# A two-layer row-and-column scan on one core: passes of one layer and eight batches, packed row steps, borders moved under the neighbouring scans

## Chip, cores and metric

The kernel runs on one core of one Trainium2 chip. The metric is the time of one execution on the device, in microseconds (us).

## What is computed

The input is 32 batches of 48 channels x 64 rows x 128 columns, float32. Each of two layers normalizes its input in 16 groups of three channels (over the group's channels, rows and columns of one batch), runs four scans over the result and adds what comes out to its input. A scan step adds a 5-tap convolution of the line before to the next line; all 48 channels mix. Down and up go along the rows with the same weights (the convolution runs along the 128 columns), right and left along the columns (the convolution runs along the 64 rows).

```
def step(w, b):
    def f(carry, inp):
        nxt = inp + _conv1d(carry, w, b)      # 48 x 48 x 5 taps, padding 2, and a bias
        return (nxt, nxt)
    return f
...
_, d_rest = jax.lax.scan(step(down_w, down_b), d0, xs[1:])        # 63 steps over rows
...
_, u_rest = jax.lax.scan(step(down_w, down_b), u0, seq)           # 63 steps back
...
_, r_rest = jax.lax.scan(step(right_w, right_b), r0, ws[1:])      # 127 steps over columns
...
_, l_rest = jax.lax.scan(step(left_w, left_b), l0, R[Ww - 2::-1]) # 127 steps back
...
x = x + _L0_conv_ref(_gn(x), ...)
x = x + _L1_conv_ref(_gn(x), ...)
```

## The kernel before

Partitions 0 to 47 hold the channels of even positions and 64 to 111 those of odd ones (`SIDES`, P = 112), so that a product of 112 x 112 weights handles two positions of a convolution at once. A chain is four batches (`G`); there are eight chains in two lanes, and `run_lane` is written as a generator, of which the loop at the end (L260 to L262) takes a step of one lane and then of the other. Each lane does its chain's first layer, the border to the second layer, the second layer and the border to the next chain, four chains one after the other.

A step (`step`, L169) is three TensorE products over the same moving line, shifted by none, one back and one ahead (L174, L175, L178), into one accumulator, and one VectorE addition of accumulator, bias and input line (L181). In down and up a line is 64 positions x 4 batches = 256 values a partition, in right and left 32 x 4 = 128. A float32 product is two passes, each with its own weight load, so every product appears as two instructions. In up, ScalarE also copies each new line to its place in the column layout (`place`, L189).

At a border (the end of `run_lane`) each of the four batches of a lane is handled in turn: GpSimd adds the scan's result to the input tile (`add_scan`, L107), SP stores it to `mid` or `out` (L104), and `stats` computes the next layer's statistics of it on VectorE (L120 to L146, with two small products L124 and L131 and a square root L136), after which `normalize` writes the map, one half on ScalarE (L153) and one on GpSimd (L160). After the second layer the tile is first loaded with a new batch (L99). Two input tiles a lane (`NX`) are loaded 25 steps ahead of the end of left (`early`). All input and output DMAs stand in SP's queue and move 512-byte runs.

The order of each engine's instructions is fixed when the program is built, from the dependences; an engine takes its queue in that order and waits where something is not ready.

Of the kernel before, what the change touches and what calls it, by code (L numbers as in the profile page):

```python
# [21 lines left out]
F32 = mybir.dt.float32  # L23
# [9 lines left out]
G = 4  # L33
LANES = 2
NX = 2
DOWN, RIGHT, LEFT = range(3)
SIDES = (slice(0, C), slice(ODD, ODD + C))
# [3 lines left out]
def kernel(  # L41
# [10 lines left out]
    HP, WP = H // 2, W // 2  # L52
    NCHAINS = B // G
    SEG = 512
    NSEG = HP * W // SEG

    cpool = ctx.enter_context(tc.tile_pool(name="cpool", bufs=1))
    carry_pool = ctx.enter_context(tc.tile_pool(name="carry", bufs=2))
    stat_pool = ctx.enter_context(tc.tile_pool(name="stat", bufs=2))
    dram = ctx.enter_context(tc.tile_pool(name="dram", bufs=1, space=bass.MemoryType.DRAM))  # L60
    ps_scan = ctx.enter_context(
        tc.tile_pool(name="ps_scan", bufs=3, space=bass.MemoryType.PSUM)
# [5 lines left out]
    w_sb = cpool.tile([P, 2, 3, 3, P], F32, tag="w_sb", name="w_sb")  # L68
    b_sb = cpool.tile([P, 2, 3], F32, tag="b_sb", name="b_sb")
    mask_sb = cpool.tile([P, P], F32, tag="mask_sb", name="mask_sb")  # L70
    xts = [
        [cpool.tile([P, HP, W], F32, tag=f"x{i}_{k}", name=f"x{i}_{k}") for k in range(NX)]
        for i in range(LANES)
    ]
    maps = [
        cpool.tile([P, WP, 2, HP, G], F32, tag=f"map{i}", name=f"map{i}")
        for i in range(LANES)
    ]
    lasts = [
        cpool.tile([P, WP, G], F32, tag=f"last{i}", name=f"last{i}") for i in range(LANES)  # L80
    ]
    mid = dram.tile([B, C, H, W], F32, tag="mid", name="mid")


    for i, t in enumerate(maps + [xt for lane in xts for xt in lane]):
        eng = nc.vector if i % 2 else nc.gpsimd
        eng.memset(t[32:64], 0.0)
    nc.scalar.dma_start(mask_sb, mask)
    nc.scalar.dma_start(b_sb, bias)
    nc.scalar.dma_start(w_sb, w)  # L90

    def rows(ap: bass.AP, b: int, side: int) -> bass.AP:
        return ap[b].rearrange("c (q r) w -> r c q w", r=2)[side]

    def load_x(lane: int, src: bass.AP, b: int) -> bass.AP:

        xt = xts[lane][b % G % NX]
        for side in range(2):
            nc.sync.dma_start(xt[SIDES[side]], rows(src, b, side))  # L99
        return xt  # L100

    def store_x(dst: bass.AP, b: int, xt: bass.AP):
        for side in range(2):
            nc.sync.dma_start(rows(dst, b, side), xt[SIDES[side]])  # L104

# [5 lines left out]
    def stats(xt: bass.AP, key: str):  # L111


        def small(n, name):
            return stat_pool.tile([P, n], F32, tag=name, name=f"{name}_{key}")
# [200 lines left out]
```

## Time and profile before

| | |
|---|---|
| median of the runs | 7141.41 us (3 runs, 7123.3 to 7152.01) |
| the profiled execution | 7140.95 us |
| its span, first to last instruction | 7139.2 us |
| mean granted TensorE clock | 0.88 |
| TensorE matmul busy | 5473.6 us (77%) |
| VectorE, ScalarE, GpSimd busy | 3006.9, 1402.4, 1279.8 us |
| moved by DMA | 258.09 MB, 497403 packets |

Busy time is that of instructions in flight; the engines overlap, so the shares don't add up to the span. PE is TensorE's matmuls, PEld its weight loads, DVE VectorE, ACT ScalarE, POOL GpSimd, SP the queue that issues most DMAs. PEclk is the clock that was granted to TensorE, as a share of 2.4 GHz. In a timeline a row's bracket tells how long the engine had been idle and whose end released it.

### The profile page before, as it was taken

How to read it: one execution, taken by the hardware profiler on the slowest of the kernel's cores; microseconds unless marked ns; L12 is line 12 of the kernel's file. 1: busy time of each engine (PE TensorE's matmuls, PEld its weight loads, DVE VectorE, ACT ScalarE, POOL GpSimd, SP SyncE). 2: the span in 40 equal slices, each digit the busy share in tenths (PEclk: the TensorE clock that was granted, in tenths of full speed). 3: DMA queues.
4: the chain of work that ended last, by engine and by line, in shares of the span. 5: the costliest groups of instructions: out<-in, count | busy, mean ns of one | idle time of the engine just before them, and what ended most of it. 6: DMA issues, size and time to landing. Idle time of an engine off the chain costs nothing. (4 is left out here: it accounts for less than half of the span.)

```text
span 7139.2 us, 85243 instructions
## 1 busy us (share of the span) xinstructions
PE 5473.6 (77%) x36736; PEld 4951.8 (69%) x36736; DVE 3006.9 (42%) x7235; ACT 1402.4 (20%) x2241; POOL 1279.8 (18%) x199
## 2 busy tenths in 40 slices
PE   3999549993399945999339994599923999459992
PEld 2889538993289943899328994489922899448992
DVE  5345523452334553345223455334522345533451
ACT  3230213201323021320122302132012230213200
POOL 5000440004400044000440004300043000530004
PEclk9999769996699976999669997799966999779996
DMA  9000350006800035000590003500058000340006
GB/s 111 1 1 1 51 91 1 1 1 88 124 1 1 1 54 88 1 1 1 89 124 1 1 1 57 85 1 1 1 89 123 1 1 1 62 80 1 1 1 106
DMA packets 497403, 258.09 MB, mean 36 GB/s; under 512 B 5392, under 2 KB 496912, under 8 KB 497024
## 3 DMA queue, kind: packets, MB, share of 16 engines
q1 hardware_dynamic: 496640, 251.68, 24.4%
q8 instruction: 287, 4.70, 0.3%
q10 hardware_dynamic: 384, 0.96, 0.1%
q14 instruction: 92, 0.75, 0.0%
HBM read 151.95 MB, written 100.66 MB: 35 GB/s over the span
## 5 line engine op out<-in xcount | busy, mean ns | idle before, releaser
L107 POOL TENSOR_TENSOR x<-x,map 112x4096 f32<-112x4096 f32 x64 | 693.6, 10850 | 5310.1 <-issue 2639.2
L124 PE MATMUL ps_stat_x<-mv_x,mask_sb 112*112 112x1 f32 x64 | 16.5, 327 | 713.9 <-DVE mv_x L122 707.9
L124 PEld LDWEIGHTS ps_stat_x<-mv_x,mask_sb 112*112 112x112 f32 x64 | 15.0, 288 | 717.4 <-DVE mv_x L122 710.4
L124 PE MATMUL ps_stat_m<-mv_m,mask_sb 112*112 112x1 f32 x64 | 16.5, 327 | 479.9 <-DVE mv_m L122 454.6
L136 ACT ACTIVATE std_m<-var_m 112x1 f32<-112x1 f32 x32 | 6.5, 203 | 1841.6 <-DVE var_m L133 1841.5
L120 DVE BATCH_NORM_STATS2 st_x<-x 112x6 f32<-112x512 f32 x256 | 155.6, 679 | 499.6 <-DMA x<-in_x 499.3
L124 PEld LDWEIGHTS ps_stat_m<-mv_m,mask_sb 112*112 112x112 f32 x64 | 15.0, 287 | 483.6 <-DVE mv_m L122 456.8
L160 POOL TENSOR_SCALAR map<-x,scale_x,offset_x 48x2048 f32<-48x2048 f32 x64 | 284.4, 4443 | 333.6 <-DVE offset_x L146 327.7
L136 ACT ACTIVATE std_x<-var_x 112x1 f32<-112x1 f32 x32 | 6.5, 203 | 1596.3 <-DVE var_x L133 1596.2
L160 POOL TENSOR_SCALAR map<-x,scale_m,offset_m 48x2048 f32<-48x2048 f32 x64 | 281.0, 4390 | 193.0 <-DVE offset_m L146 169.1
L120 DVE BATCH_NORM_STATS2 st_m<-x 112x6 f32<-112x512 f32 x256 | 160.5, 679 | 348.3 <-POOL x L107 348.3
L153 ACT ACTIVATE map<-x,offset_x,scale_x 48x2048 f32<-48x2048 f32 x64 | 282.8, 4419 | 43.8 <-DVE offset_x L146 40.3
L153 ACT ACTIVATE map<-x,offset_m,scale_m 48x2048 f32<-48x2048 f32 x64 | 280.5, 4383 | 50.5 <-DVE offset_m L146 33.1
L189 ACT COPY map<-last 48x256 f32<-48x256 f32 x32 | 12.9, 403 | 1251.8 <-DVE last L181 1251.5
L131 PE MATMUL ps_stat_m<-sq_m,mask_sb 112*112 112x1 f32 x64 | 16.6, 329 | 153.1 <-DVE sq_m L130 153.1
L131 PEld LDWEIGHTS ps_stat_m<-sq_m,mask_sb 112*112 112x112 f32 x64 | 14.3, 285 | 157.1 <-DVE sq_m L130 157.1
L130 DVE SCALAR_TENSOR_TENSOR sq_m<-dev_m,mv_m 112x1 f32<-112x1 f32 x32 | 78.1, 2439 | 0.7
L181 DVE SCALAR_TENSOR_TENSOR map<-ps_1L0r,b_sb,map 112x128 f32<-112x128 f32 x127 | 44.6, 351 | 44.6 <-PE ps_1L0r L178 44.6
L181 DVE SCALAR_TENSOR_TENSOR map<-ps_7L0r,b_sb,map 112x128 f32<-112x128 f32 x127 | 44.6, 351 | 44.5 <-PE ps_7L0r L178 44.5
L181 DVE SCALAR_TENSOR_TENSOR map<-ps_5L0r,b_sb,map 112x128 f32<-112x128 f32 x127 | 44.6, 351 | 44.5 <-PE ps_5L0r L178 44.5
L181 DVE SCALAR_TENSOR_TENSOR map<-ps_3L0r,b_sb,map 112x128 f32<-112x128 f32 x127 | 44.6, 351 | 44.3 <-PE ps_3L0r L178 44.3
L181 DVE SCALAR_TENSOR_TENSOR map<-ps_3L1r,b_sb,map 112x128 f32<-112x128 f32 x127 | 44.6, 351 | 44.2 <-PE ps_3L1r L178 44.2
(617 smaller groups left out, 17240.0 us busy)
## 6 DMA issues: line engine op xcount, KB each, us to landing
x<-in_x SPq DMA_DIRECT2D x128, 768.0 KB, 16.2
mid<-x SPq DMA_DIRECT2D x64, 768.0 KB, 12.0
x<-mid SPq DMA_DIRECT2D x64, 768.0 KB, 16.1
out<-x SPq DMA_DIRECT2D x64, 768.0 KB, 12.6
w_sb<-in_w ACTq DMA_DIRECT2D x1, 882.0 KB, 12.3
mask_sb<-in_mask ACTq DMA_DIRECT2D x1, 49.0 KB, 1.9
b_sb<-in_b ACTq DMA_DIRECT2D x1, 2.6 KB, 5.4
```

Of the source, the lines that this page charges most:

```text
L107: nc.gpsimd.tensor_tensor(xt, xt, maps[lane][:, :, :, :, j].rearrange("c p r q -> c q (p r)"), ALU.add)
L120: nc.vector.bn_stats(st[:, s, :], flat[:, bass.ts(s, SEG)])
L124: nc.tensor.matmul(ps[:, 0:1], mask_sb, mv[:, 0:1], start=True, stop=True)
L130: nc.vector.scalar_tensor_tensor(sq, dev, dev, mv[:, 1:2], ALU.mult, ALU.add)
L131: nc.tensor.matmul(ps[:, 1:2], mask_sb, sq, start=True, stop=True)
L136: nc.scalar.activation(std, var, AF.Sqrt)
L153: nc.scalar.activation(maps[lane][SIDES[0], :, hs, :, j], view[hsl, :, 0, :], AF.Identity, bias=offset[hsl], scale=scale[hsl],)
L160: nc.gpsimd.tensor_scalar(maps[lane][SIDES[1], :, hs, :, j], view[hsl, :, 1, :], scale[hsl], offset[hsl], ALU.mult, ALU.add,)
L181: nc.vector.scalar_tensor_tensor(dst, ps, b_sb[:, layer, way : way + 1], inp, ALU.add, ALU.add)
L189: nc.scalar.copy(maps[lane][SIDES[hs], :, ws, q, :], carry[SIDES[ws]])
```

## The change

The work is cut differently. A pass is one layer of eight batches (`GB`), and there are eight passes: four of the first layer, then four of the second. There is one chain at a time.

- Down and up: eight neighbouring positions of a line x 48 channels are packed into 384 = 3 x 128 partitions (`PIECES`, `NG`), so a line is three groups of 128 values. A step (`row_step`) is nine 128 x 128 products in the order of `PRODUCTS` (input group, output group, shift) into three accumulators, with one VectorE addition for each group behind its last product. Results are written in place.
- Right and left: as before, but the two interleaved chains are the two halves of the eight batches (`col_step`).
- Rows and columns share one region (`arena`): the rows begin at its start, the columns 20 rows later (`SHIFT`). In up, each eight finished rows are moved to the column layout by 20 DMAs (`hand_over`); ScalarE's copies are gone.
- `prepare` brings eight batches of x to DRAM in the order that the rows want (load, statistics, GpSimd reordering, store, in 16 pieces); it runs for the first eight batches ahead of everything and for the others while a pass of the first layer is in right. `fetch` loads rows by ten DMAs and normalizes them in place by 24 ScalarE activations.
- The rows 0 to 19 of the next pass are loaded during left (three `fetch`). The residual of a pass (`drain`, 16 pieces) and the other six `fetch` are written among the down steps of the next pass. In the first layer a piece of the residual adds on GpSimd, stores to `mid` and computes statistics; in the second it adds and stores to `out`.
- Weights of the row steps are placed by 62 DMAs a layer, on ScalarE's queue at the start and on SP's during right of the fourth pass.

The new functions, cut to their core, and the driving loop (`collect` is one statistics instruction for each batch; `scaling` is the work of `stats` for eight batches at once, with four small products; the functions `load_x`, `store_x`, `add_scan`, `stats`, `normalize`, `step`, `place`, `scan` and `run_lane` go):

```
-G = 4
-LANES = 2
-NX = 2
+GB = 8
+HB = GB // 2
+E8 = 8
+FULL = 128
+NG = E8 * C // FULL
+SHIFT = 20
+CH = 2
+RB = 8
+LOADS = tuple(slice(a, b) for a, b in ((0, 4), (4, 12), (12, 20))) + tuple(
+    slice(a, min(a + 8, 64)) for a in range(20, 64, 8)
+)
+EARLY = 3
+PRODUCTS = (
+    (0, 0, 0),
+    (0, 1, 0),
+    (1, 0, 0),
+    (1, 1, 0),
+    (2, 0, -1),
+    (2, 1, 0),
+    (1, 2, 0),
+    (0, 2, 1),
+    (2, 2, 0),
+)
...
+    arena = const([FULL, SHIFT * ROW + HP * PAIR], "arena")
+    rows = arena[:, 0 : H * ROW].rearrange("p (h o n) -> p h o n", h=H, o=NG)
+    cols = arena[0:P, SHIFT * ROW :].rearrange(
+        "p (q e k b) -> p q e k b", q=HP, e=E8, k=NK
+    )
...
+    def prepare(g: int):
...
+        for j in range(NCH):
+            nat, perm = nats[j % 2], perms[j % 2]
...
+                nc.sync.dma_start(
+                    nat[SIDES[s]],
+                    x[g * GB : (g + 1) * GB, :, h : h + CH].rearrange(
...
+            collect(st, j, nat, f"x{g}_{j}")
...
+            for r in range(CH):
+                nc.gpsimd.tensor_copy(perm5[:, r], nat[:, r])
...
+                nc.sync.dma_start(
+                    stages[0][g][h : h + CH].rearrange("h c n -> c h n"), perm[SIDES[s]]
+                )
+            yield
+        return scaling(st, f"x{g}")
+
+    def fetch(layer: int, g: int, j: int, scale, offset):
+
+        hs = LOADS[j]
+        src = stages[layer][g][hs].rearrange("h c (e n) -> e c h n", e=E8)
+        for e, c0, c1, o, p0 in PIECES:
+            nc.sync.dma_start(rows[p0 : p0 + c1 - c0, hs, o], src[e][c0:c1])
+        view = rows[:, hs].rearrange("p h o (k b) -> p o b h k", b=GB)
+        for o in range(NG):
+            for b in range(GB):
+                nc.scalar.activation(
...
+    def hand_over(j: int):
+
+        qs = slice(RB // 2 * j, RB // 2 * (j + 1))
+        for r in range(2):
+            src = rows[:, RB * j : RB * (j + 1)].rearrange("p (q r) o n -> r o p q n", r=2)
+            dst = cols[SIDES[r], qs].rearrange("p q e k b -> e p q (k b)")
+            for e, c0, c1, o, p0 in PIECES:
+                nc.sync.dma_start(dst[e][c0:c1], src[r, o][p0 : p0 + c1 - c0])
+
+    def residual(layer: int, g: int, q: int, i: int, st):
...
+        for r in range(2):
+            nc.sync.dma_start(nat[SIDES[r]], src[r, :, q : q + CH])
+        res = cols[:, q : q + CH].rearrange("p q e k b -> p q (e k b)")
+        if layer == 0:
+            nc.gpsimd.tensor_tensor(res, res, nat, ALU.add)
...
+                nc.sync.dma_start(dst[r, :, q : q + CH], res[SIDES[r]])
+            collect(
...
+        else:
+            for t in range(CH):
+                nc.gpsimd.tensor_tensor(
+                    perm[:, t].rearrange("p (b k e) -> p b k e", b=GB, k=NK),
...
+    def row_step(layer: int, key: str, prev, inp, dst):
...
+        for n, (i, o, s) in enumerate(PRODUCTS):
+            seen[o] += 1
+            a, b = max(0, -s) * GB, N - max(0, s) * GB
+            nc.tensor.matmul(
+                ps[o][:, a:b],
+                wd[:, n],
+                prev[:, i, a + s * GB : b + s * GB],
...
+            if seen[o] == left[o]:
+                nc.vector.scalar_tensor_tensor(
+                    dst[:, o], ps[o], bd[:, layer, o : o + 1], inp[:, o], ALU.add, ALU.add
+                )
...
+    def drain(n: int):
...
+        first = (H - SHIFT) * ROW // (CH * PAIR) + 1
+        order = list(range(first)) + list(range(NCH - 1, first - 1, -1))
+        loads = list(range(EARLY, len(LOADS))) if n + 1 < len(passes) else []
+        for i, j in enumerate(order):
+            residual(layer, g, CH * j, i, st)
+            free = SHIFT + (i + 1) * CH * PAIR // ROW
+            while loads and (i >= first or LOADS[loads[0]].stop <= free):
+                fetch(*passes[n + 1], loads.pop(0), *coeffs[passes[n + 1]])
+            yield
+        if layer == 0:
+            coeffs[1, g] = scaling(st, f"m{g}")
...
+    load_row_weights(0, nc.scalar)
+    load_col_weights(0, nc.scalar)
+    for _ in drive(prepare(0), (0, 0)):
+        pass
+    for j in range(len(LOADS)):
+        fetch(0, 0, j, *coeffs[0, 0])
+
+    for n, (layer, g) in enumerate(passes):
...
+        for stage, i in scans(n):
+            if stage in ("down", "up") and left_over:
+                t = i if stage == "down" else 2 * H - 2 - i
+                due = t % 2 == 0 if t <= 18 else t % 6 == 0
+                if due and next(left_over, "end") == "end":
+                    left_over = None
+            if stage == "right":
+                if ahead and i % 7 == 0 and next(ahead, "end") == "end":
+                    ahead = None
+                if i == 1 and nxt and nxt[0] != layer:
+                    load_row_weights(nxt[0], nc.sync)
+            if stage == "left" and nxt and i % 32 == 31 and i < 96:
+                fetch(*nxt, 2 - i // 32, *coeffs[nxt])
+        if nxt and nxt[0] != layer:
+            load_col_weights(nxt[0], nc.sync)
+    for _ in drain(len(passes) - 1):
+        pass
```

## Rows read from the trace of the kernel before

**Rows 1.** The page's 40 slices, in tenths: granted clock, DMA engines.
```profile
PEclk9999769996699976999669997799966999779996
DMA  9000350006800035000590003500058000340006
```

**Rows 2.** Table of stretches: head, rows, columns, border, border, tail; column names first.
```profile
core 0: us, PE busy (x) PEld busy (x) DVE busy (x) ACT busy (x) POOL busy (x), PEclk, DMA share, GB/s
0.00:135.60 135.60, 20.95 (x59) 14.09 (x59) 91.16 (x151) 67.12 (x25) 85.60 (x23) 1.00 1.23 128
135.60:459.20 323.60, 322.94 (x1487) 265.18 (x1488) 119.25 (x247) 105.97 (x255) 4.12 (x1) 1.00 0.08 9
459.20:800.20 341.00, 340.61 (x3049) 340.19 (x3047) 178.35 (x508) 0.99 (x3) 0.04 (x1) 1.00 0.00 1
800.20:1001.50 201.30, 23.83 (x66) 15.76 (x65) 89.09 (x150) 67.77 (x24) 152.71 (x23) 0.51 0.61 97
...
1663.30:1917.10 253.80, 20.93 (x59) 14.12 (x59) 60.92 (x149) 69.21 (x24) 154.24 (x24) 0.51 0.95 141
7008.20:7139.20 131.00, 0.00 (x1) 0.00 (x0) 0.35 (x1) 0.00 (x0) 86.59 (x8) 0.52 0.87 144
```

**Rows 3.** Timeline of a step in right: start us, us, engine, line, operation.
```profile
600.23 0.38 PE L178 MATMUL ps_1L0r<-map,w_sb 112*112 112x124 f32 x2
...
600.44 0.38 PE L174 MATMUL ps_0L0r<-map,w_sb 112*112 112x128 f32 x2
...
600.65 0.35 DVE L181 SCALAR_TENSOR_TENSOR map<-ps_1L0r,b_sb,map 112x128 f32<-112x128 f32 x1 [0.35 <-PE ps_1L0r L178]
600.66 0.38 PE L175 MATMUL ps_0L0r<-map,w_sb 112*112 112x124 f32 x2
...
601.05 0.27 PEld L174 LDWEIGHTS ps_1L0r<-map,w_sb 112*112 112x112 f32 x2
```

**Rows 4.** The page's groups (busy us, mean ns), and one of down.
```profile
L107 POOL TENSOR_TENSOR x<-x,map 112x4096 f32<-112x4096 f32 x64 | 693.6, 10850 | 5310.1 <-issue 2639.2
L160 POOL TENSOR_SCALAR map<-x,scale_x,offset_x 48x2048 f32<-48x2048 f32 x64 | 284.4, 4443 | 333.6 <-DVE offset_x L146 327.7
L189 ACT COPY map<-last 48x256 f32<-48x256 f32 x32 | 12.9, 403 | 1251.8 <-DVE last L181 1251.5
L181 DVE SCALAR_TENSOR_TENSOR map<-ps_1L0r,b_sb,map 112x128 f32<-112x128 f32 x127 | 44.6, 351 | 44.6 <-PE ps_1L0r L178 44.6
...
L181 DVE SCALAR_TENSOR_TENSOR map<-ps_1L0d,b_sb,map 112x256 f32<-112x256 f32 x46 | 22.3, 484 | 36.7 <-PE ps_1L0d L178 36.7
```

**Rows 5.** Timeline at a border's end: lane 0 scans again, lane 1 is not ready.
```profile
976.21 10.89 POOL L107 TENSOR_TENSOR x<-x,map 112x4096 f32<-112x4096 f32 x1
...
979.62 0.48 DVE L181 SCALAR_TENSOR_TENSOR map<-ps_0L1d,b_sb,map 112x256 f32<-112x256 f32 x1 [2.97 <-PE ps_0L1d L178]
...
987.14 4.84 DVE L120 BATCH_NORM_STATS2 st_m<-x 112x6 f32<-112x512 f32 x8 [7.04 <-POOL x L107]
991.90 0.47 DVE L181 SCALAR_TENSOR_TENSOR map<-ps_0L1d,b_sb,map 112x256 f32<-112x256 f32 x1
...
992.42 1.19 PE L174 MATMUL ps_0L1d<-map,w_sb 112*112 112x256 f32 x2 [9.39 <-DVE map L181]
```

**Rows 6.** Timeline at the start of that border: GpSimd's additions, VectorE's small operations.
```profile
800.15 43.27 POOL L107 TENSOR_TENSOR x<-x,map 112x4096 f32<-112x4096 f32 x4 [660.43 <-issue]
...
822.73 0.63 DVE L120 BATCH_NORM_STATS2 st_m<-x 112x6 f32<-112x512 f32 x1
...
824.11 8.53 DVE L128 TENSOR_TENSOR dev_m<-mv_m,mean_m 112x1 f32<-112x1 f32 x1
```

**Rows 7.** The page's DMA queues (packets, MB, share), and the timeline of one issue.
```profile
q1 hardware_dynamic: 496640, 251.68, 24.4%
q8 instruction: 287, 4.70, 0.3%
...
1.16 0.45 ACTq L89 DMA_DIRECT2D b_sb<-in_b  x1
```

**Rows 8.** Table of stretches, columns as in rows 2: lane 0 alone, then both lanes.
```profile
996.60:1001.40 4.80, 4.07 (x8) 2.14 (x8) 0.69 (x3) 4.45 (x2) 4.38 (x1) 0.50 0.86 171
...
1004.80:1011.00 6.20, 5.19 (x23) 3.62 (x23) 2.27 (x5) 0.59 (x1) 0.85 (x1) 0.99 1.14 163
```

More of the change, by code (lines that the diff above doesn't have):

```diff
@@ L177, in step @@
         )
         nc.tensor.matmul(
-            ps[:, 0 : n - 1], wt[:, 2], prev[:, 1:n], start=False, stop=True
+            ps[:, 0 : HP - 1], wt[:, 2], prev[:, 1:HP], start=False, stop=True
         )
         nc.vector.scalar_tensor_tensor(
-            dst, ps, b_sb[:, layer, way : way + 1], inp, ALU.add, ALU.add
+            dst, ps, bc[:, layer, way : way + 1], dst, ALU.add, ALU.add
         )
-    def place(lane: int, h: int, carry: bass.AP):
-        q, hs = divmod(h, 2)
-        for ws in range(2):
-            nc.scalar.copy(maps[lane][SIDES[hs], :, ws, q, :], carry[SIDES[ws]])
@@ L191, in scan @@
-    def scan(lane: int, layer: int, key: str, early):
-        m, last = maps[lane], lasts[lane]
-        def row(h):
-            return m[:, :, h % 2, h // 2, :]
-        def col(v):
-            return m[:, v // 2, v % 2, :, :]
-        for h in range(1, H):
-            dst = row(h) if h < H - 1 else last
-            step(lane, layer, DOWN, f"{key}d{h}", row(h - 1), row(h), dst)
-            yield
-        place(lane, H - 1, last)
-        prev = last
+    passes = [(layer, g) for layer in range(2) for g in range(NGRP)]
@@ L211, in scan @@
[L211 to L215 removed]
+            row_step(
+                layer, f"{key}u{h}", rows[:, h + 1], rows[:, h - 1] if h else end, rows[:, h]
+            )
+            if h % RB == 0:
+                hand_over(h // RB)
+            yield "up", h
         for v in range(1, W):
[L217 removed]
@@ L260 @@
-    lanes = [run_lane(i) for i in range(LANES)]
-    while lanes:
-        lanes = [lane for lane in lanes if next(lane, "end") != "end"]
+            for half in range(2):
+                col_step(layer, LEFT, half, f"{key}l{v}{half}", v + 1, v)
+            yield "left", v
+    load_row_weights(0, nc.scalar)
[5 more added lines that the diff above has]
+    for n, (layer, g) in enumerate(passes):
+        nxt = passes[n + 1] if n + 1 < len(passes) else None
+        left_over = drain(n - 1) if n else None
+        ahead = None
+        if nxt and nxt[0] == 0:
+            ahead = drive(prepare(nxt[1]), nxt)
+        for stage, i in scans(n):
[6 more added lines that the diff above has]
+                if ahead and i % 7 == 0 and next(ahead, "end") == "end":
+                    ahead = None
+                if i == 1 and nxt and nxt[0] != layer:
[4 more added lines that the diff above has]
+            load_col_weights(nxt[0], nc.sync)
```

307 lines of the change are left out of this document (171 added, 136 removed).

## Prediction

> **What bounds the kernel now.** I read three views: the 40 slices of the page, a table of stretches cut where the stages change, and the timeline inside three of the stretches. In the slices the granted clock is full through each scan and falls at each border, where the DMA engines are busy instead [rows 1]. The table puts numbers to it [rows 2]. A layer of two chains is a row stage (down and up, 126 steps of two lanes) of 323.6 us, in which TensorE is busy for 322.9, and a column stage (right and left, 254 steps) of 341.0 us, busy for 340.6. Both are TensorE at its rate. Between them lie seven borders: four like 800 to 1001 (201.3 us) and three like 1663 to 1917 (253.8 us), in which TensorE works about 10% of the time, with 135.6 us ahead and 131.0 us behind. 8 x (323.6 + 341.0) + 4 x 201.3 + 3 x 253.8 + 135.6 + 131.0 = 7150, the span of 7139.2 but for a few us of overlap. So 1833 us are borders and ends, 5317 us scans. The profiled execution took 7140.95 us, 1.75 more than its span and 0.5 less than the median of the runs; I add 2 to sums of spans.
>
> **Row steps.** Two lanes of three products of 256 columns become one chain of nine products of 128 columns (two of them 120): 1152 columns where 1536 were. In the column stage a 128-column product follows the next in 0.22 us (600.44 to 600.66) [rows 3]. Nine make **1.98 us** where 323.6 / 126 = 2.57 stood. One chain has nobody to hide its additions, so the order of the products must. A product of two passes ends 0.38 us after its start (600.23), VectorE begins 0.04 later (600.65), takes 0.35, and the next weight load starts 0.05 after that (601.05) [rows 3]. With products at 0.22: group 0 is complete at 0.88 + 0.38 = 1.26, added by 1.65, wanted by the next step at 1.98; group 1 is complete at 1.48, has to wait for VectorE until 1.65, is added by 2.0 and its bank wanted at 2.20; group 2 is complete at 2.14, added by 2.53, wanted at 2.86. Each has 0.15 us or more to spare, so no wait. Rows with strided operands already run at rate: the 256-wide addition takes 484 ns against 351 for 128 [rows 3, 4], 1.04 ns a value either way, and the matmuls of both stages keep TensorE full [rows 2]. 8 x 126 x 1.98 = **1996 us**. The column step keeps its shapes: 8 x 341 = **2728**.
>
> What no row shows is a 128-column weight load in such a stream. Weight loads are busy 340 of 341 us in the column stage and 265 of 324 in the row stage [rows 2], so in the former they may be what sets the 341 / (254 x 12) = 112 ns a pass. If their time goes with 128 / 112 columns, a pass takes 128 ns, a step 2.30 and the sum grows by 323 us; if not, nothing. I take nothing, since the 0.22 us is within 3% of twice the 107 ns that half a 256-column pass of the row stage takes (323.6 us / 1512 passes = 214 ns).
> The Trainium skill ("TensorE: Matmul & The Clock Gate", LDWEIGHTS) gives a weight load as its columns divided by 1.2, in ns: 107 for 128. By that, load and matmul tie, and an estimate from it lies at the lower of my two ends; no row here shows such a load.
>
> **The ends.** The tail handles the same eight maps and bytes as now: 131. The head moves the first eight batches twice before a scan can begin (to DRAM in the new order, then in by rows): 25.2 MB at the 144 GB/s of 512-byte packets (251.68 MB in 24.4% of 16 engines x 7139 us) or at some 220 GB/s of the 16 KB packets (4.70 MB in 0.3%) [rows 7] is 114 to 175 us, of which GpSimd's reordering is beside it (32 copies of 1024 values, at 2.2 to 2.65 ns a value 72 to 87 us [rows 4]); then scaling, one load of four rows and its 24 activations, 20 us. Since the second load needs only its first rows, I take **150** (130 to 195).
>
> **Borders moved under scans.** Seven of them, 1567 us now, turn into these:
> - Hand-over. Each up scan sends its rows to the column layout in 8 x 20 DMAs on SP's queue. An issue costs 0.45 us [rows 7], so 20 take 9 us, and 1.57 MB at 144 GB/s takes 11. Seven of the eight lie under the next eight steps (16 us); the right scan starts only when the last has landed. 14 us (3, if it is quick, to 25 with a backlog) x 8 = **112**.
> - DMA issues altogether: 160 hand-over + 90 load + 64 to 96 residual + 64 prepare = up to 410 a pass, 185 us of SP in about 600: no bound by themselves, but they stand in one queue behind each other's waits. The 62 weight DMAs of the second layer go under a right scan.
> - Residual of a layer-0 pass (four): 16 pieces, each a load, a GpSimd addition of 2048 values (10.85 us for 4096, so 5.4 [rows 4]), a store, and 8 statistics of 256 values. The statistics run on VectorE ahead of the scan's additions: 512 values cost 4.84 / 8 = 0.6 us [rows 5], 256 some 0.34; 128 of them are 44 us if all lie on the chain, 13 if each falls in a gap of the row step, in which VectorE is busy 3 x 0.35 of 1.98. Worse is what they wait for. At 987 lane 1's statistics stood in VectorE's queue waiting for GpSimd, lane 0's finished step behind them, and TensorE lost 9.4 us [rows 5]. The order of the queues is evidently made from estimated times and not as the code is written (lane 1's statistics between lane 0's chain at 822 [rows 6]), and there it counted GpSimd too fast. Under the down scan nine pieces and six row loads must pass first: 9/16 of 25.2 MB at 220 to 144 GB/s, 64 to 98 us, + 8.65 MB of rows at 144, 60 us, = 124 to 158 us beside a scan of 125. I take 40 for statistics and 45 for holds, **85** a pass (15 to 160), x 4 = **340**.
> - Residual of a layer-1 pass (three): no statistics; the wait is that of the rows 20 to 63 for the same transfers. **40** (0 to 100) x 3 = **120**.
> - Preparing the next eight batches (three passes): 16 pieces of 8 statistics, 13 to 44 us, and 25.2 MB beside the hand-overs' 12.6. **50** (10 to 110) x 3 = **150**.
> - Seven scalings with four small matmuls and some ten small VectorE operations, queued among the scan's own; those with two SBUF operands stood for a whole GpSimd addition (8.53 us at 824 [rows 6]), while the scan's own addition, with one operand in PSUM, kept its 0.48 beside a running one (979.62 in 976.21 to 987.10 [rows 5]). **8** (4 to 25) x 7 = **56**.
> Activations (216 a pass, under 0.4 us each by the 403 ns for 256 values [rows 4]) make under 90 us of an idle ScalarE: nothing, unless rows come late.
>
> Sum: 1996 + 2728 + 150 + 131 + 112 + 340 + 120 + 150 + 56 = 5783, with 2 around it **5785 us**.
>
> **The rivals.**
> 1. All hidden: statistics in gaps, no holds, quick hand-overs. 5005 for scans and ends + 24 + 7 x 13 + 28 = 5150 to 5450. For it: VectorE is half idle. Against it: the hold at 987 [rows 5].
> 2. Weight loads set the pass: 5785 + 323 = 6108.
> 3. The clock: it stays at 1.2 GHz while TensorE has small gaps. Lane 0 alone ran at 0.50 from 996.6 to 1001.4 although TensorE was busy 4.07 of 4.80 us, and full clock returned after both lanes had filled it [rows 8]. If statistics and late rows keep the seven shared down scans there, 7 x 63 steps cost twice: + 873, 6658. Against it: by itself the step has no gap, and 2.7 us of statistics come only every other step at worst.
> 4. Slower than before: the borders aren't hidden, because VectorE's queue serialises them. If each of the 64 + 48 pieces with statistics holds the scan for its whole chain, 1.57 MB at 144 (10.9) + 5.4 + 2.7 = 19 us, that is 2128 in place of 490: 7423. It decides from 16.5 us a piece on. For it: the same hold [rows 5]; against it: two buffers let a load run beside the addition ahead of it, which leaves the larger of the two.
>
> **How the numbers follow.** Forecast (5500 to 6100) 0.40; all hidden 0.15; weight loads 0.15; clock 0.12; more backlog than I allow, 6100 to 6650 by the upper bounds of holds and hand-overs, 0.10; slower 0.08. The range, 5250 to 6650, leaves out the best of the first rival, half of the clock's and the last: 0.2. A measurement of this kernel tells about 0.5% from no change; within it 0.01, so faster 0.91, slower 0.08.
>
> **What would show it.** Row steps of 1.98 us at full clock in the up scans, where no border disturbs them (2.30: weight loads; near 4: clock); column stages of 341; TensorE idle some 14 us ahead of each right scan, released by a DMA; VectorE waiting for GpSimd at statistics in layer-0 down scans and nowhere in layer 1's. The forecast is wrong if a down scan beside a residual takes over 300 us, if VectorE's share of the row step is longer than 0.35 an addition, or if transfers between SBUF regions run well below 144 GB/s.

## The result, and the profile after

The changed kernel takes **6102.35 us** (median of 4 runs, 6102.06 to 6106.58) where the kernel before, run beside it, took 7141.03: a ratio of 0.8549, 95% interval 0.8531 to 0.8567, or 1039 us less. The forecast was 5785 in a range of 5250 to 6650. So the sign and the size are about right, and the changed kernel is 317 us slower than the working said. A rewrite of the order of its DMAs and of the place of its statistics, found below, takes it to 5254.

The 40 slices of the page of after (granted clock and DMA engines in tenths) answer [rows 1]. The borders with idle scans are gone, the DMA engines work beside the scans, and the clock dips a little nearly everywhere instead of deeply at seven places:

```profile
PEclk9999998999989999899988999889999799898985
DMA  6636246552464533632065401642045500642014
```

The table of stretches of after answers [rows 2]. First the head; then pass 01 (layer 0, second group of eight batches) cut into down, up, the wait between up and right, right, and left; then pass 11 (layer 1) the same way, and the tail:

```profile
core 0: us, PE busy (x) PEld busy (x) DVE busy (x) ACT busy (x) POOL busy (x), PEclk, DMA share, GB/s
0.00:182.50 182.50, 2.01 (x8) 1.81 (x8) 57.16 (x153) 4.81 (x11) 96.55 (x37) 1.00 0.66 148
814.10:1006.00 191.90, 150.11 (x1137) 146.87 (x1137) 101.62 (x269) 71.08 (x144) 45.16 (x10) 0.87 0.62 126
1006.00:1169.40 163.40, 139.47 (x1143) 137.95 (x1141) 90.28 (x257) 0.22 (x1) 27.53 (x7) 0.93 0.49 117
1169.40:1178.30 8.90, 0.02 (x1) 0.05 (x1) 0.35 (x1) 0.00 (x0) 0.00 (x0) 0.71 0.47 114
1178.30:1405.40 227.10, 194.19 (x1533) 191.08 (x1533) 132.82 (x401) 2.57 (x7) 63.81 (x32) 0.91 0.65 135
1405.40:1575.80 170.40, 170.40 (x1529) 170.40 (x1528) 89.10 (x255) 31.65 (x67) 0.00 (x0) 1.00 0.06 8
3767.10:3947.40 180.30, 140.82 (x1138) 138.44 (x1137) 61.74 (x189) 71.19 (x144) 76.89 (x20) 0.87 0.62 127
3947.40:4074.00 126.60, 126.60 (x1135) 126.46 (x1133) 60.52 (x189) 0.00 (x0) 46.69 (x13) 1.00 0.48 113
4074.00:4132.50 58.50, 0.05 (x1) 0.02 (x1) 0.35 (x1) 0.00 (x0) 0.00 (x0) 0.53 0.49 120
...
5887.30:6100.30 213.00, 0.01 (x1) 0.00 (x0) 0.35 (x1) 0.00 (x0) 117.75 (x32) 0.51 0.46 111
```

Where nothing disturbs it, a row stage half is 126.6 to 126.8 us (the up scan of pass 11) and a column scan 170.4, both with TensorE busy throughout at full clock. Everything above that is a border that shows through. Two rows look odd. The down scan of pass 11, whose VectorE has no statistics to do (61.7 us busy, the scan's own additions alone), takes nearly as long as that of pass 01 with its statistics. And the wait ahead of right is 58.5 us in layer 1 but 8.9 in layer 0. Added up, down, up and wait come to 361.6 to 370.5 us **in all seven passes with a residual, in both layers**, where 253.6 would be free of waits. That looks like one cause for both layers. The runs below show otherwise: layer 1 loses it to the queue alone, layer 0 mostly to the statistics, and the sums happen to agree.

The timeline of SP's queue (start, time of the issues, operation) at the end of the down scan and through the up scan of pass 11 shows a candidate. L283 loads a piece of the residual, L305 stores one, L276 is the hand-over, L257 the next pass's rows:

```profile
3955.57 4.66 SPq L305 DMA_DIRECT2D out<-perm  x4
3960.27 1.22 SPq L283 DMA_DIRECT2D nat<-mid  x2
3969.55 4.65 SPq L305 DMA_DIRECT2D out<-perm  x4
...
4026.31 4.66 SPq L305 DMA_DIRECT2D out<-perm  x4
4031.03 105.18 SPq L276 DMA_DIRECT2D arena<-arena  x156
```

A store waits for its addition, and the load of the next piece but one stands behind the store. So load, addition and store take turns, 14 us a piece (3955.57 to 3969.55), though there are two buffers. The hand-over of the rows stands behind the last store: 156 of its 160 DMAs go out in one go from 4031, long after the up scan had made most of them possible, at 105.18 / 156 = 0.67 us each. The right scan waits for them until 4132.5.

The tail, alone on the chip, shows the same order in GpSimd's additions (L298) and SP's queue:

```profile
5914.66 4.49 SPq L305 DMA_DIRECT2D out<-perm  x4
5919.19 1.23 SPq L283 DMA_DIRECT2D nat<-mid  x2
5924.73 7.36 POOL L298 TENSOR_TENSOR perm<-arena,nat 112x1024 f32<-112x1024 f32 x2 [6.44 <-DMA nat<-mid]
```

GpSimd adds for 7.36 us and then stands 6.44 for a load that was issued only when the stores were out.

The groups of the page (busy us, mean ns, idle before) answer [rows 4]: the two residual additions, the two kinds of statistics, and a scaling:

```profile
L298 POOL TENSOR_TENSOR perm<-arena,nat 112x1024 f32<-112x1024 f32 x128 | 486.8, 3832 | 2304.1 <-DVE arena L352 1809.3
L286 POOL TENSOR_TENSOR arena<-arena,nat 112x2048 f32<-112x2048 f32 x64 | 288.7, 4529 | 1635.8 <-DVE arena L352 1072.6
L261 ACT ACTIVATE arena<-arena,offset_x,scale_x 128x128 f32<-128x128 f32 (+1 forms) x864 | 419.6, 583 | 771.9 <-DMA arena<-xin 730.6
L177 DVE BATCH_NORM_STATS2 st_m<-arena 112x6 f32<-112x256 f32 x512 | 273.7, 605 | 17.7 <-POOL arena L286 17.7
L177 DVE BATCH_NORM_STATS2 st_x<-nat 112x6 f32<-112x256 f32 x512 | 179.7, 411 | 116.7 <-DMA nat<-in_x 113.8
```

The statistics of the residual, st_m, read every eighth value and take 605 ns; those of the input, st_x, lie side by side and take 411. VectorE waited for GpSimd at statistics for 17.7 us in the whole run, so the holds that I feared from [rows 5] happen for some 4 us a pass. What happens instead is in the timeline of VectorE and of TensorE in the down scan of pass 01, a piece's eight statistics in one block:

```profile
857.36 0.35 DVE L331 SCALAR_TENSOR_TENSOR arena<-row_01d,bd,arena 128x128 f32<-128x128 f32 x1 [0.29 <-PE row_01d L323]
858.46 0.61 DVE L331 SCALAR_TENSOR_TENSOR arena<-row_01d,bd,arena 128x128 f32<-128x128 f32 x2 [0.76 <-PE row_01d L323]
858.99 4.23 DVE L177 BATCH_NORM_STATS2 st_m<-arena 112x6 f32<-112x256 f32 x8
...
866.12 0.35 DVE L331 SCALAR_TENSOR_TENSOR arena<-row_01d,bd,arena 128x128 f32<-128x128 f32 x1 [0.93 <-PE row_01d L323]
...
863.53 5.69 PE L323 MATMUL row_01d<-arena,wd 128*128 128x120 f32 x25 [3.31 <-DVE arena L331]
```

Before the block VectorE stands idle 0.29 and 0.76 us in every row step. The block takes 4.23 us at once, TensorE waits 3.31, and the first steps after it run slower: VectorE's gap at 866 is 0.93 where 0.29 stood. The table of two stretches, before the block and behind it, gives the reason, the granted clock:

```profile
850.00:858.90 8.90, 8.90 (x82) 8.90 (x81) 4.27 (x14) 0.00 (x0) 4.88 (x2) 1.00 0.37 88
863.50:867.50 4.00, 3.97 (x18) 3.98 (x19) 1.05 (x3) 0.00 (x0) 0.00 (x0) 0.50 0.83 154
```

It is full, 2.4 GHz, while TensorE is busy without a break, and 0.50, 1.2 GHz, after the idle 3.31 us; a step of 18 passes takes 4.0 us there. Not every such gap is followed by it: behind an idle 3.37 us at 1048 in the up scan of this pass the clock is granted in full (1.00 from 1048.35 to 1052.00). The 0.87 of the whole down scan is a mean of the two.

### The profile page after: what moved, and what is told of

The parts are those of the page before. It is cut to its first block, busy times and chain, and to the rows that moved or that the text cites. A ratio compares the mean times of both kernels' runs of the same rounds, so it can differ in the third digit from the quotient of the medians.

```text
span 6100.3 us, 102555 instructions
## 1 busy us (share of the span) xinstructions
PE 5016.6 (82%) x42592; PEld 4979.0 (82%) x42592; DVE 2870.0 (47%) x8277; ACT 843.3 (14%) x1737; POOL 1067.5 (17%) x333
## 5 line engine op out<-in xcount | busy, mean ns | idle before, releaser
L298 POOL TENSOR_TENSOR perm<-arena,nat 112x1024 f32<-112x1024 f32 x128 | 486.8, 3832 | 2304.1 <-DVE arena L352 1809.3
L261 ACT ACTIVATE arena<-arena,offset_m,scale_m 128x128 f32<-128x128 f32 (+1 forms) x864 | 420.6, 584 | 2203.6 <-DMA arena<-mid 1298.0
L286 POOL TENSOR_TENSOR arena<-arena,nat 112x2048 f32<-112x2048 f32 x64 | 288.7, 4529 | 1635.8 <-DVE arena L352 1072.6
L261 ACT ACTIVATE arena<-arena,offset_x,scale_x 128x128 f32<-128x128 f32 (+1 forms) x864 | 419.6, 583 | 771.9 <-DMA arena<-xin 730.6
L243 POOL COPY perm<-nat 112x1024 f32<-112x1024 f32 x128 | 254.3, 2021 | 904.6 <-DMA nat<-in_x 683.3
L177 DVE BATCH_NORM_STATS2 st_m<-arena 112x6 f32<-112x256 f32 x512 | 273.7, 605 | 17.7 <-POOL arena L286 17.7
L177 DVE BATCH_NORM_STATS2 st_x<-nat 112x6 f32<-112x256 f32 x512 | 179.7, 411 | 116.7 <-DMA nat<-in_x 113.8
L323 PE MATMUL row_10d<-arena,wd 128*128 128x128 f32 x1134 | 149.6, 300 | 44.4 <-DVE arena L331 39.1
L323 PE MATMUL row_02d<-arena,wd 128*128 128x128 f32 x1134 | 149.9, 300 | 44.0 <-DVE arena L331 38.9
L323 PE MATMUL row_01d<-arena,wd 128*128 128x128 f32 x1134 | 150.2, 301 | 41.8 <-DVE arena L331 37.6
```

Of the source, the lines that this page charges most:

```text
L177: nc.vector.bn_stats(st[:, b, j, :], t[:, b])
L243: nc.gpsimd.tensor_copy(perm5[:, r], nat[:, r])
L261: nc.scalar.activation(view[:, o, b], view[:, o, b], AF.Identity, bias=offset[:, o, b : b + 1], scale=scale[:, o, b : b + 1],)
L286: nc.gpsimd.tensor_tensor(res, res, nat, ALU.add)
L298: nc.gpsimd.tensor_tensor(perm[:, t].rearrange("p (b k e) -> p b k e", b=GB, k=NK), cols[:, q + t].rearrange("p e k b -> p b k e"), nat[:, ...
L323: nc.tensor.matmul(ps[o][:, a:b], wd[:, n], prev[:, i, a + s * GB : b + s * GB], start=seen[o] == 1, stop=seen[o] == left[o],)
```

## The experiments

Theory A: the blocks of statistics, with the slower clock behind them, are what the row stages of layer 0 lose. Theory B: the order of SP's queue sets the row stage of both layers, the tail and part of the head. The first runs set them against each other.

**Without the residual's statistics.** Of the 16 pieces one keeps them, and the scaling reads that one.

```diff
-            collect(st, i, cols[:, q : q + CH]..., f"m{g}_{i}")
+            if i == 0:
+                collect(st, i, cols[:, q : q + CH]..., f"m{g}_{i}")
```

> Leaves out 15 of 16 pieces of the statistics of the second layer's input (the second layer is scaled by the first piece's); everything else stays. Now a layer-0 residual takes 365 to 370 us from the start of down to the start of right, 112 to 117 above the 253 of two undisturbed row stages. Theory A (as predicted: VectorE's statistics hold the scan): nearly all of that goes, some 4 x 100, run about 5700 us. Theory B (SP's queue sets the end: pieces of 14 us one behind the other and then 160 hand-over issues of 0.67 us): down and up get shorter, but the right scan has to wait the longer for the last hand-over, some 50 us instead of 9; it gains 10 to 20 us a pass, run 6020 to 6070 us.

5860.78 us (5855 to 5863), between the two. The table of pass 02 (down, up, wait):

```profile
1518.80:1669.20 150.40, 134.90 (x1145) 133.57 (x1144) 71.88 (x217) 71.33 (x145) 45.13 (x10) 0.93 0.76 161
1669.20:1796.00 126.80, 126.79 (x1136) 126.60 (x1134) 60.59 (x189) 0.00 (x0) 27.49 (x7) 1.00 0.54 128
1796.00:1827.60 31.60, 0.00 (x0) 0.03 (x1) 0.35 (x1) 0.00 (x0) 0.00 (x0) 0.55 0.50 122
```

Down falls by 43 us and up by 41, and the wait ahead of right grows from 8.6 to 31.6: part of the gain is given back to the hand-over, which becomes the later one. Both causes act, one behind the other.

**Hand-over on ScalarE's queue.**

```diff
-                nc.sync.dma_start(dst[e][c0:c1], src[r, o][p0 : p0 + c1 - c0])
+                nc.scalar.dma_start(dst[e][c0:c1], src[r, o][p0 : p0 + c1 - c0])
```

> The 160 hand-over DMAs of a pass go to ScalarE's queue instead of SP's; nothing else. Theory A with bandwidth behind the waits: no change beyond 20 us, since bytes and statistics stay. Theory B: in the three passes with a layer-1 residual the hand-overs no longer stand behind the residual's stores; only the rows whose columns are still occupied wait, so TensorE's idle time ahead of right falls from 58 us to 15 to 30; in the four with a layer-0 residual up loses less to it, 9 us to 5; run 5950 to 6020 us.

6044.80 us (6038 to 6053), a gain of 58 where B expected 80 to 150. The wait in layer 1 fell from 58 only to 40 to 47 us: freed of the stores, the DMAs are still 160 in one queue, and cost no less there (90 of them in 70.72 us, 0.79 each). Moving them didn't touch the 14 us a piece either. It did move the preparation of passes 00 to 02: part of its statistics now stands in up, which grew by 15 to 32 us, while right fell to 186, 177 and 177.

**Loads ahead of the stores.** The load of the piece after next is written between a piece's addition and its stores; nothing else changes.

```diff
+        load(0)
+        load(1)
         for i, j in enumerate(order):
-            residual(layer, g, CH * j, i, st)
+            residual(layer, g, CH * j, i, st, lambda: load(i + 2))
...
             nc.gpsimd.tensor_tensor(res, res, nat, ALU.add)
+            load_ahead()
             dst = stages[1][g].rearrange("(q r) c n -> r c q n", r=2)
```

> A piece's load is written ahead of the stores of the piece two before it, so that it no longer stands behind them in SP's queue; same DMAs, same operations. Theory B: a piece's pace falls from 14 us (landing 5.5 + addition 7.4 + issues) to 8 to 9 (addition alone); the tail falls from 213 to about 140 us, the wait ahead of right in the layer-1 passes from 58 to under 20, their down scans from 180 to 140 to 160, layer-0 passes by 20 to 40 each; run 5600 to 5800. Theory A: tail as in B, the layer-0 passes as now, run about 5900 to 5950. If the DMA engines were the bound of a piece, it would change nothing.

5664.42 us (5659 to 5669): 438 us less, by an order of DMAs alone. Pass 11 (down, wait) and the tail:

```profile
3681.10:3808.00 126.90, 126.90 (x1137) 126.74 (x1136) 60.88 (x189) 71.55 (x144) 85.20 (x22) 1.00 0.89 203
...
3934.80:3955.10 20.30, 0.03 (x1) 0.06 (x1) 0.35 (x1) 0.00 (x0) 0.00 (x0) 0.57 0.49 119
...
5531.40:5657.40 126.00, 0.04 (x1) 0.00 (x0) 0.35 (x1) 0.00 (x0) 117.55 (x32) 0.52 0.84 187
```

The layer-1 residual now costs the down scan nothing, and the tail is 126.0 us with GpSimd busy for 117.6 of them, so it is GpSimd's. That is B for layer 1 and the tail. Layer 0 keeps 343 to 346 a row stage.

**The same order in the preparation, and hand-overs on both queues** (one side on SP's, one on ScalarE's).

```diff
...
-                nc.sync.dma_start(dst[e][c0:c1], src[r, o][p0 : p0 + c1 - c0])
+                (nc.sync, nc.scalar)[r].dma_start(dst[e][c0:c1], src[r, o][p0 : p0 + c1 - c0])
```

> e3, and the same order in the preparation, and the hand-overs shared by SP's and ScalarE's queues. Theory B: as e3, and the wait ahead of right falls to about 5 to 9 us in every pass, the head by some 40 us (a pair of pieces took 17.6 us there); run 5480 to 5650. Theory A: statistics still hold four passes, some 5800.

5470.61 us (5459 to 5476). The head is 152.6, the wait ahead of right 2.2 to 6.3 us in every pass, and the row stages of layer 1 are 255.9 to 256.5 against 253.6 free of waits. Only layer 0 is left: 337 to 343 us. Pass 02 (down, up):

```profile
1475.60:1657.70 182.10, 146.39 (x1137) 144.01 (x1136) 109.65 (x285) 71.33 (x144) 54.41 (x12) 0.90 0.67 148
1657.70:1812.70 155.00, 138.88 (x1143) 137.63 (x1142) 86.90 (x258) 0.22 (x1) 26.58 (x9) 0.93 0.54 120
```

**Without the statistics of the input** (the kernel after, 15 of 16 pieces of batches 8 to 31 left out).

> The changed kernel, leaving out 15 of 16 pieces of the statistics of x in the three preparations under right (batches 8 to 31 are scaled by their first piece's); the preparation's copies and transfers stay. Right is now 196 us in the first pass and 227 and 229 in the next two, against 172 to 173 undisturbed. If statistics on VectorE are the cost: right falls to 173 to 180 in all three, run 5960 to 5990. If VectorE waiting for loads that stand behind stores is the cost: the same fall, as a wait needs an instruction that waits; what tells the two apart is the run with the loads written ahead and the statistics kept, where right fell only to 197: 25 of 55 us are then the statistics' own time and 30 the wait.

5980.59 us (5973 to 5989), as expected. The right scans with a preparation, 195.9, 227.1 and 229.0 us in after, fall to 172.5, 177.5 and 177.8. So it is the statistics there, again, and nearly nothing of the preparation's 25 MB or of GpSimd's copies. But it is their place and not their number, as traces of runs that keep them all show. These are TensorE's waits for VectorE in the right scan of pass 02 (us in total, times, longest), in after and in the last run below:

```profile
PE col_02r L345 <- DVE arena L352: 27.8, 15, 2.0
PE col_02r L355 <- DVE arena L362: 1.4, 3, 0.9
```

In VectorE's timeline of after 15 blocks of eight statistics stand in that scan, one for each wait. With both queues mended 7 blocks are left, the other statistics stand singly between column steps (and some in up), and right takes 197 us; in the run that then leaves out the residual's statistics it is 9 blocks and 209 us, in the last run no block, 91 statistics by ones and twos, and 175. The wait for loads that I expected for 30 of the 55 us isn't there: VectorE waited for no load ahead of a statistic in these scans of after. The runs differ in other things too, and none changed the blocks alone.

**Statistics written two to a row step, and the input's one to a column step.** On the kernel with both queues mended; the second of the two also cuts the first memset to the columns that need it. In both, some of the residual's statistics are taken after the next pass's rows have been loaded over their values.

> e4 (loads ahead, hand-overs on two queues), and the residual's statistics are written two to a row step instead of eight behind each other; same instructions. In e4 the four layer-0 residuals still cost 82 to 87 us each: 16 pieces of 5.2 us, of which VectorE's eight statistics are 4.2. If the cost is the block of eight that the scan can't pass, with the clock that falls behind it: spread, each fits a gap in part (VectorE has 0.9 us a step free, two statistics take 1.1), and a pass loses 20 to 45; run 5260 to 5390. If it is VectorE's time as such, 128 x 0.53 = 68 a pass stays: run 5400 to 5450. If it is the clock alone, almost nothing stays: 5150 to 5200.

> e6, the preparation's statistics one to a step of right, and a memory clear at the start that covers only the part that the row scans don't write first (15872 of 40448 values, 13 us of GpSimd instead of 34). Right falls from 197 to 180 to 185 in two passes, the head by some 15 to 20 us: 40 to 55 us less than e6.

5453.82 (5450 to 5455) and 5455.39 us (5452 to 5459): 17 and 15 us less than the kernel they start from, all of it in the right scans (187 to 192 for 197); the row stages of layer 0 stay at 340 to 346. But neither is a test, for the statistics aren't spread. The timeline of VectorE in pass 02 of the first shows them in blocks as before, for the queue doesn't keep the order in which the code is written:

```profile
1514.86 8.41 DVE L441 BATCH_NORM_STATS2 st_m<-arena 112x6 f32<-112x256 f32 x16
```

The second also shows that the 34 us memset of the head, smaller now, was no term of its own: the head is 147.7 against 150.3.

**The mended queues without the residual's statistics**, to size what they cost once the queue is out of the way.

> The kernel of e4_all_queue that leaves out 15 of 16 pieces of the residual's statistics of layer 0 (its second layer is scaled by the statistics of one piece). e4_all_queue still spends 343.0, 343.3, 337.0 and 338.9 us in the row stages of layer 0 that carry a residual, where those of layer 1 take 255.9 to 256.5. Theory: the 16 blocks of eight statistics, with the slower clock after each, are all that is left there. Then the four row stages fall to 255 to 260 and the time to 5470.6 - 336 = 5135 us (5110 to 5160). Rival: GpSimd's additions, the stores and the loads behind them hold a part as well: row stages of 275 to 310, 5200 to 5340 us.

5228.47 us (5220 to 5236). The row stages fell from 343.0, 343.3, 337.0 and 338.9 to 280.0, 275.5, 270.5 and 278.0 us: **64.5 us a pass for the statistics left out**, 0.54 us for each of 120. Some 20 stay, so the theory that they were all of it missed, and the rival's ranges held. The trace doesn't show the rival's cause, though. Pass 02 (down, up), and what stands in its down scan:

```profile
1419.10:1561.60 142.50, 133.15 (x1144) 132.11 (x1143) 71.70 (x217) 71.23 (x145) 54.39 (x12) 0.95 0.80 189
1561.60:1688.40 126.80, 126.80 (x1136) 126.67 (x1135) 60.56 (x189) 0.00 (x0) 19.00 (x6) 1.00 0.60 138
...
1424.25 1.67 DVE L177 BATCH_NORM_STATS2 st_m<-arena 112x6 f32<-112x256 f32 x3 [2.56 <-POOL arena L296]
...
1467.24 4.51 POOL L296 TENSOR_TENSOR arena<-arena,nat 112x2048 f32<-112x2048 f32 x1 [11.83 <-DMA nat<-xin]
1467.29 4.50 DVE L212 TENSOR_TENSOR t_m<-var_m,r_m 128x24 f32<-128x24 f32 x1
...
1473.06 2.29 PE L337 MATMUL row_02d<-arena,wd 128*128 128x120 f32 x9 [5.06 <-DVE arena L345]
```

Up is undisturbed. Down is 15.7 us over, in two places. At its start, some 5 us: the statistics of the first piece, which this run keeps, wait for GpSimd's addition. At step 19, some 10 us: the scaling, which here needs that piece alone and so comes early. Its operation L212, with two operands in SBUF, stands for a whole GpSimd addition, and TensorE for 5.06 us. The rest of the 20 is a wait ahead of right of 6.1 us in place of some 2. So what stays in the scan is a hold and a scaling, not loads or stores, and the theory was nearer than its miss says.

The rows also price the slower clock. Down and up of pass 02 are 67.8 us shorter than with the statistics. 42.5 of these are time in which TensorE stood idle; the other 25.3 are time in which it was busy with the same products (146.39 and 138.88 us with the statistics, 133.15 and 126.80 without), most of it the slower clock, which was granted as 0.90 and 0.93 there and as 0.95 and 1.00 here. The right scans of passes 01 and 02 took back some 11 us each (208 and 209).

**Statistics really spread.** A small copy of the row just added, on VectorE, goes to the place that a pair of statistics then overwrites. The pair so depends on its row step and can't come earlier. The pieces are due every 4 to 5 row steps, the next pass's rows only after their pieces' statistics.

```diff
...
+                to, view = pending.pop(0)
+                nc.vector.tensor_copy(to, rows[0:P, newest[0], 0, 0:12].rearrange("p (b k) -> p b k", b=2))
+                for b in range(2):
+                    nc.vector.bn_stats(to[:, b], view[:, b])
```

> e4_all_queue with all its statistics, two of them a row step: a small copy on VectorE out of the row just added into the place of the statistics ties each pair to its step, so that they can't gather in a block. They run a piece or two behind the additions. Rows of after: three additions of 0.35 us in a step of 2.01 us leave VectorE gaps of 0.76 and 0.29 us. Theory of the block: two statistics of 0.53 us and a copy of 0.16 us make a step with them 2.3 us at most, some 0.3 us over, so 64 x 0.3 = 19 us a pass in place of 84, and the clock holds: row stages of 270 to 290 us, 5180 to 5290 us in all. Rival, that VectorE's time as such counts, wherever it stands: 128 x 0.53 + 64 x 0.16 = 78 us a pass, 5430 to 5500 us.

> As e9_two_a_step8, with the statistics up to three pieces behind the additions in place of two: fewer of them are left in groups of four to eight (2 groups of eight a pass), but the last two loads of the next pass's rows come some 10 us later. Theory of the block: within 20 us of e9_two_a_step8, lower if the groups count (each costs 4 us and the slower clock after it), higher if the loads come too late for the scan. Rival as there: 5430 to 5500 us.

5418.91 us (5396 to 5427) and 5403.67 (5393 to 5409). The theory of the block predicted 5180 to 5290 and seemed to fall; the rival's 5430 to 5500 was missed as well. The trace of the second says otherwise. Its up scan of pass 02 is 135.8 us where 155.0 stood, with the clock at full, but down is 198.6, and most of the gain on 5470.61 is in the right scans of passes 01 and 02 (175 us for 197). In down, the timeline of VectorE and of GpSimd reads:

```profile
1558.60 3.56 DVE L404 COPY st_m<-arena 112x12 f32<-112x12 f32 x1
...
1557.62 4.51 POOL L296 TENSOR_TENSOR arena<-arena,nat 112x2048 f32<-112x2048 f32 x1 [0.91 <-DMA nat<-xin]
```

A copy of twelve values takes 0.16 us as a rule, and here 3.56. The addition of GpSimd that began at 1557.62 ends at 1562.13, the copy at 1562.16. Of 256 copies 48 took over a microsecond, 156 us in all, and each of the 48 ends within 0.2 us of the end of a GpSimd addition, while 44 statistics that lie wholly inside such additions took 0.60 to 0.64 us as everywhere. The experiment's own tie cost what the spreading gained. So it was made again without a copy.

```diff
-                nc.vector.tensor_copy(to, rows[0:P, newest[0], 0, 0:12].rearrange("p (b k) -> p b k", b=2))
                 for b in range(2):
+                    nc.vector.bn_stats(to[:, b], rows[0:P, newest[0], 0, 0:8])
                     nc.vector.bn_stats(to[:, b], view[:, b])
```

> e9_two_a_step12 with another tie: in place of the small copy, two statistics of 8 values of the row just added, written to the place that the real ones then overwrite. In the trace of e9_two_a_step12 a row step with two statistics and a copy of 0.16 us takes 2.2 us, against 2.01 without, but 64 copies of a pass are 48.1 us busy, 0.16 us for most and 2.7 to 4.4 us for those that began during one of GpSimd's 4.5 us additions; each of these ends where the addition ends. Theory: copies that wait for GpSimd, not statistics, cost e9_two_a_step12 its gain, and a statistic, which has one operand in SBUF, doesn't wait. Then 48.1 - 10 = 38 us a pass are gone, and up to 10 more with the slower clock behind them, while two tiny statistics of 0.16 us take 0.15 us a step more: row stages of 285 to 305 us in layer 0, 5200 to 5280 us in all. Rival, that VectorE's statistics cost as much however they stand: row stages of 330 to 345, 5390 to 5440 us.

**5254.04 us** (5249 to 5261), a ratio of 0.7359 to the kernel before (0.7347 to 0.7371) and 848 us below the changed kernel. The theory held. Pass 02 (down, up), and a step of its down scan in VectorE's timeline:

```profile
1408.40:1569.20 160.80, 141.56 (x1137) 136.34 (x1136) 112.40 (x363) 71.22 (x144) 68.04 (x15) 0.94 0.83 192
1569.20:1703.30 134.10, 132.59 (x1144) 129.46 (x1142) 98.83 (x324) 0.22 (x1) 20.99 (x10) 1.00 0.59 135
...
1421.77 0.23 DVE L405 BATCH_NORM_STATS2 st_m<-arena 112x6 f32<-112x8 f32 x2
1422.03 0.64 DVE L406 BATCH_NORM_STATS2 st_m<-arena 112x6 f32<-112x256 f32 x1
...
1422.84 0.61 DVE L406 BATCH_NORM_STATS2 st_m<-arena 112x6 f32<-112x256 f32 x1
...
1424.02 0.23 DVE L405 BATCH_NORM_STATS2 st_m<-arena 112x6 f32<-112x8 f32 x2
```

A step with two statistics and two ties takes 2.25 us (1421.77 to 1424.02) against 2.01 without: 0.24 us where two statistics in a block take 1.06 (4.23 / 4). In such a step the same work on the same engine costs a quarter of it, since it stands in the gaps of the chain. Over a pass the row stages of layer 0 are 298 to 299 us, against a mean of 276 without the statistics: 22 us in place of 64.5. This run also spaces the pieces and loads the rows later than the one with the queues mended, and no run has that without statistics, so the 22 are not the price of the place alone. Of the 217 us below that run 169 are in the four row stages, and 41 in the right scans of passes 01 and 02, where no block of statistics is left.

## Why the prediction was right, and where it was off

The sum was 5783 and the span is 6100.3. By its own terms (from the stages of all eight passes, of which the table above shows two):

- **Row and column steps: right.** An undisturbed row step is 126.8 / 63 = 2.013 us (1.98 forecast), a column stage 172.5 + 170.4 = 343 (341): 4773 us in place of 4724, + 47. The step's order of work is as argued: at full clock VectorE waits 0.29 and 0.76 us a step for TensorE, and TensorE for nothing. The rival of the weight loads falls: a pass of 128 columns takes 2.013 us / 18 = 112 ns, as one of 112 columns did, where 128 ns and a step of 2.30 were its price. Whether loads or matmuls set the 112 ns is not shown, for both are busy throughout (126.46 and 126.60 us of 126.60). The clock rival falls as it was priced: undisturbed scans hold full clock, and disturbed down scans have 0.87 in the mean, not 0.5.
- **Head** 182.5 (150), + 33, **tail** 213.0 (131), + 82, **hand-over waits** 2.1 to 8.9 in layer 0 and 57 to 59 in layer 1, 212 in all (112), + 100, and the **layer-1 residual** 157 over (120), + 37. These four are some 250 of the 317 us, and one step of the prediction failed in all of them. I wrote that SP's 410 issues were "no bound by themselves, but they stand in one queue behind each other's waits", and then priced the queue by issue times and the transfers by bytes. The wait of a store for its addition holds the next load, and that makes 14 us a piece out of three things that could overlap. An issue between SBUF regions also took 0.67 us and not 0.45, and the sign that I named came: while TensorE waits for them, the hand-overs move 114 to 120 GB/s and not 144. With the loads ahead of the stores, and the hand-overs split, head and tail are 152.6 and 125.9, the waits 2 to 6 us, the layer-1 down scans 127: the forecast's terms, or better. The tail in particular was taken over from before as "the same eight maps and bytes", without a look at its order.
- **Layer-0 residual:** 421 us in four passes (340), + 81, with the wrong make-up. I had 40 us a pass of statistics and 45 of holds, in which statistics wait for GpSimd. VectorE waited 17.7 us for GpSimd at them in the whole run. The statistics cost 64.5 us a pass, as the runs with mended queues measured, with and without them: they take 605 ns where their values lie eight apart (I had 0.34 us, from [rows 5], where they lie side by side), and they come eight at a time, so that hardly any fall into gaps. That too little for statistics and too much for holds came near together is luck. The rest, with the queue's share, is B's: 364 to 370 us became 337 to 343 when the order of DMAs changed.
- **Preparation:** 134 us (150), plus 10 in pass 00's row stage; right in size. By the run without the input's statistics it is nearly all theirs, and by the traces that of their blocks; I had 13 to 44 us a pass for them and the rest for transfers.
- **Scalings:** 56 forecast as a term, - 56, for what they cost stands inside the two terms above. TensorE's waits in after show it, with 12 us more in the right scans with a preparation:

```profile
PE ps_m L185 <- DVE mv_m L183: 24.8, 4, 6.2
```

  So they cost some 37 us in idle time, and the forecast was near. The wait that I had named, of two-operand work for GpSimd, is not the one that counts in after (L212 took 0.17 to 0.18 us in all eight scalings): TensorE's first small product (L185) stands for the end of the statistics.
- **Rival "slower"** needed 16.5 us a piece, all of it on the chain. The piece took 14 us, near that, but off TensorE's path except where rows or the hand-over came late: loads and additions of the residual run beside the scan even when they run one after another among themselves.

So the forecast was low by 317 us, some 250 of them because of a queue that it named and didn't price. Once that queue is mended and the statistics are spread, "all hidden" (5150 to 5450) is where the kernel stands: 5254 us with every statistic in.

Not settled: the row stages of layer 0 are still some 42 us above the 256 of layer 1 at 5254 us. By TensorE's waits 16 to 17 us of that are places in the down scan where the scan's additions come late (16.9 us in 7 waits in pass 02); no run took them away.

## What to carry to other kernels

When work is moved under a chain, price its queues by who waits in them, not by issue times or bytes: write the loads for the next piece ahead of the stores that wait for this one, and count what stands behind each wait. Work on an engine that a chain needs at every step is cheap in the chain's gaps, and in a block costs most of its time and a slower clock behind it; that an engine is half idle says nothing until the order of its queue is known, and where a scheduler sets that order, a real dependency on the step is what holds a piece of work in its place. An experiment's own helper must be priced as well, as the copy that waited for GpSimd shows.

## What the runs showed of the hardware

- A DMA between two regions of SBUF cost 0.67 us of SP's queue (105.18 us for 156), and 0.79 on ScalarE's; loads from DRAM cost 0.40 to 0.62 there. None of these is a fixed price: while ScalarE's queue made those copies, a load of rows on SP's cost 2.07 (74.41 us for 36). I had 0.45 for all [rows 7].
- GpSimd's addition of 1024 values takes 3832 ns when it also puts them in another order, and 4529 for 2048 that lie as they are. From before I had worked out 5.4 for 2048 [rows 4]. The Trainium skill ("GPSIMD Engine Reference", 3.1 Elementwise) gives 4497 ns for 2048 fp32 values; this trace agrees with 4529.
- A copy on VectorE with source and target in SBUF waits for a GpSimd addition that runs, to its end (all 51 copies that began inside one), while statistics and the scan's additions, with one input in SBUF, don't (44 statistics inside additions at 0.60 to 0.64 us). The Trainium skill ("SBUF — State Buffer", Who interferes with whom) says that copies may enter a mode that takes the port pair VectorE shares with GpSimd, and that an instruction with at most one SBUF input outside such modes doesn't contend; the traces agree. My prediction knew only the case of two operands, from [rows 6].
- Statistics of 256 values take 605 ns when the values lie eight apart and 411 when they lie side by side; a scaling of 128 values takes 583 ns on ScalarE, where I had assumed under 400.
